# Row sums of a third head group by accumulating transfers, with a new instruction order and buffers named in lists

## The chip, the cores and the metric

The kernel runs on one core of a Trainium2 chip. A core has five engines that run side by side, each with its own queue of instructions that it takes in order: TensorE (PE, matrix products into the PSUM memory), VectorE (DVE, element-wise work and statistics), ScalarE (ACT, functions of one input), GpSimd (POOL, here small operations and the issue of some transfers) and SyncE (SP, here only the issue of transfers). Transfers (DMA) run on 16 engines that all queues share. Engines wait for one another through semaphores.

The metric is the device time of one execution in microseconds. Before the change it is 3014.59 us, the median of three runs (3012.68 to 3015.29).

## The reference

There are 32 graphs of 512 nodes with 256 features. For each, two layers of masked attention over the same adjacency matrix are computed. Layer 0 is a whole transformer block (attention, layer norm, a two-layer perceptron of width 1024, layer norm) inside a residual and another norm; layer 1 is attention alone inside a residual and a norm. Cut to what matters here:

```python
allowed = (adj > 0) | (adj.T > 0) | eye            # layer 0; layer 1: adj != 0
scores = einsum('hqd,hkd->hqk', q * scale, k)      # 8 heads of 32
attn = softmax(where(allowed, scores, -inf), -1)
ctx = einsum('hqk,hkd->hqd', attn, v)
x = layernorm(x + ctx @ Wo.T + bo)
ff = relu(x @ W1.T + b1) @ W2.T + b2               # layer 0 alone
```

The softmax is computed as exp(scores), multiplied by the mask, divided by its sum over the keys. That row sum, 512 queries by 8 heads for each layer of each graph, is what the change moves.

## The kernel before

Everything of a graph is held transposed: scores have the keys on the 128 partitions and the queries along the free side. A layer of a graph is worked in eight steps `k`, two head groups `hg` of four heads by four blocks of 128 keys. A step has four parts. `scores(layer, k)` (line 404) writes the four heads' scores into the one PSUM tile `s`. `exp` (line 413) has ScalarE write their exponentials into an SBUF tile `p` of 128 x 2048 fp32, of which there are eight. `masked` (line 417) has VectorE multiply it by the mask. `product` (line 424) has TensorE multiply it by the values, summing over the four key blocks of a group in the PSUM tile `acc`.

The row sums go another way, to spare TensorE. After a product, `pair(layer, k)` (line 437) has GpSimd issue a transfer of 1 MB that adds tile `k + 1` onto tile `k`. `fold` (line 440) is the same addition on VectorE. Per layer there are three pairs, (0,1), (2,3) and (4,5), and three folds: 0 onto 2 ends group 0 in tile 2; 6 + 7 into tile 3 and then 4 onto tile 3 end group 1 in tile 3 (whose own content was summed by then). So one tile per group, `2 + hg`, holds sums over four key blocks, and what is left is the sum over 128 partitions. There are two ways for that:

- `sums` (line 448): TensorE multiplies the tile by a matrix of ones, four matmuls into a PSUM tile `psR`, which comes out already spread over 32 partitions a head; `blocks` (line 489) has VectorE transpose it in blocks of 32.
- for groups that are in `SPREAD`: two accumulating transfers (`halve`, line 464) add the upper half of the partitions onto the lower, 128 to 64 and 64 to 32. Four copies (`spread`, line 469, on SyncE's queue) put the four heads next to each other on the partitions of the tile `part`, of which there is one. `blocks` transposes that, and `reduce` (line 493) sums the 32 values on VectorE.

In both cases `invert` (line 498), `widen` (line 506) and `divide` (line 510) follow on VectorE, and `guard` (line 502) on GpSimd adds the sums to a running total that is looked at once, at the end. Then `project` (psO) and the rest of the layer follow. `SPREAD` holds (layer 0, group 0) and (layer 1, group 0). The last graph's layer 1 has no transfers at all: its `sums` takes the four tiles of a group straight, 16 matmuls, which `final` decides.

The order of all work is written out by hand as three lists of calls, which are issued as they stand: `opening` (five graphs), `period` (run 26 times, each time for five neighbouring graphs, `a` the oldest, `c` in the middle of its layer 0 and its perceptron, `d` at its first attention, `e` being loaded), and `closing`. A call puts its instructions at the end of its engine's queue, so that a list is an order for each of the five queues. A list therefore says both what follows what on an engine and, roughly, what stands beside it on the others.

Buffers come from pools. A tile is named by a tag and a key, and the pool hands out the buffers of a tag in turn (`p` has eight, `y` four, `x`, `xT`, `v`, `kT` two). Only the three PSUM banks for dense products are named one by one, in a string of digits, `banks`. A new tile in a buffer waits for all readers of the old one. Dense products (line 162) are made either `wide`, one matmul with 128 columns, or as four matmuls with 32 columns each, which lie side by side in the array.

Of the kernel before, what the change touches and what calls it, by code (L numbers as in the profile page):

```python
# [27 lines left out]
def kernel(ctx: ExitStack, tc: tile.TileContext, t: dict, out: bass.AP):  # L28
# [15 lines left out]
    P = 128  # L44
# [106 lines left out]
    def plain(pools: ExitStack):  # L151
# [7 lines left out]
        def dense(out, lhsT, rhs, start, stop, wide):  # L159
# [4 lines left out]
        SPREAD = {(0, 0), (1, 0)}  # L164

        banks = iter(
            "012012021021122121012012010210210210201012102021121021012012012012102102102102102020120122021201212101120120212010"
            + "120121212010121212012012120120021212102101010212101010210210102102201010" * 13
            + "102120201210021021010210102102102021201021010210202101201201210210212102102102121021021021021021202102120120"
        )  # L170
# [5 lines left out]
        class Graph:  # L176
# [6 lines left out]
            def at(self, tag, n, shape, dtype=F32, **kw):  # L183

                key = (tag, n)
                if key not in self.tiles:
                    name = f"{tag}_{self.b}" + "".join(f"_{i}" for i in (n if isinstance(n, tuple) else () if n is None else (n,)))
                    pool = small if tag in SMALL else ps_s if tag == "s" else ps_a if tag == "acc" else work
                    self.tiles[key] = pool.tile([P, *shape], dtype, tag=tag, name=name, **kw)
                return self.tiles[key]  # L190

            def bank(self, kind, n, shape):

                key = (kind, n)
                if key not in self.tiles:
                    name = f"ps{kind}_{self.b}" + "".join(f"_{i}" for i in n)
                    self.tiles[key] = ps_d.tile([P, *shape], F32, tag=f"d{next(banks)}", name=name, bufs=1)
                return self.tiles[key]

            def final(self, layer):  # L200

                return self.b == B - 1 and layer == 1
# [239 lines left out]
            def sums(self, layer, hg):  # L442

                ps = self.bank("R", (layer, hg), [N])
                folded = [2 + hg] if not self.final(layer) else range(hg * NQ, (hg + 1) * NQ)
# [11 lines left out]
            def spread_out(self, layer, hg):  # L457

                return (layer, hg) in SPREAD and not self.final(layer)

# [125 lines left out]
        def opening(a, b, c, d, e):  # L586
# [6 lines left out]
            b.flip(1)  # L593
            b.sort(1, 0, 0)
            a.entries()
            a.transpose(0, 0)
            a.transpose_out(0, 0)
            a.query_key(0, 0, 0, None, wide=True)
# [3 lines left out]
            b.cast()  # L602
            a.query_key(0, 1, 0, None, wide=True)
            a.query_key_out(0, 1, 0, None)
            a.entry(0)
            a.entry(2)
            a.masks(0)
            a.scores(0, 3)
            a.exp(0, 3)
            a.scores(0, 2)  # L610
            a.exp(0, 2)
            a.query_key(0, 1, 1, None)
            b.flip(0)
            a.scores(0, 0)
            a.exp(0, 0)
            a.masks(1)
            a.masks(2)
            a.value(0, 0)
            a.value_out(0, 0)
            a.scores(0, 1)  # L620
            b.sort(1, 0, 1)
            a.exp(0, 1)
            a.query_key(0, 0, 1, None)
            a.query_key_out(0, 1, 1, None)
            a.query_key_out(0, 0, 1, None)
            a.value(0, 1)
            a.masked(0, 0)
            b.sort(1, 1, 0)
            a.value_out(0, 1)
            a.masked(0, 1)  # L630
            a.scores(0, 5)
            a.exp(0, 5)
            a.constants(22, 23)
            a.product(0, 0)
            a.pair(0, 0)
            a.constants(4, 6)
            a.once(0)
            b.sort(0, 1, 0)
            a.product(0, 1)
            b.sort(0, 0, 0)  # L640
            a.masked(0, 2)
            a.constants(10, 12)
            a.masked(0, 3)
            b.sort(1, 1, 1)
            a.scores(0, 4)
            a.exp(0, 4)
            a.masked(0, 4)
            a.scores(0, 6)
            b.sort(0, 1, 1)
            b.join(0, 1)  # L650
            a.exp(0, 6)
            a.product(0, 2)
            a.scores(0, 7)
            a.exp(0, 7)
            a.masked(0, 7)
            a.product(0, 3)
            a.context(0, 0)
            b.join(1, 0)
            b.sort(0, 0, 1)
            a.pair(0, 2)  # L660
            a.fold(0, 2, 2, 0)
            a.product(0, 4)
            a.once_out(0)
            a.bias(1)
            b.join(0, 0)
            b.entry(0)
            b.value(0, 0)
            b.join(1, 1)
            b.query_key(0, 1, 0, None)
            a.halve(0, 0, P // 2)  # L670
            b.query_key(0, 0, 0, None)
            b.query_key_out(0, 0, 0, None)
            b.query_key_out(0, 1, 0, None)
            b.query_key(0, 1, 1, None)
            b.scores(0, 0)
            b.value(0, 1)
            a.halve(0, 0, P // 4)
            b.exp(0, 0)
            a.masked(0, 5)
            a.product(0, 5)  # L680
            b.value_out(0, 1)
            b.query_key(0, 0, 1, None)
            a.masked(0, 6)
            b.scores(0, 2)
            a.fold(0, 3, 6, 7)
            a.product(0, 6)
            a.product(0, 7)
            a.pair(0, 4)
            b.exp(0, 2)
            a.fold(0, 3, 3, 4)  # L690
            a.constants(20, 22)
            b.query_key_out(0, 1, 1, None)
            a.constants(6, 8)
            a.spread(0, 0, 0)
            b.query_key_out(0, 0, 1, None)
            b.scores(0, 3)
            a.spread(0, 0, 1)
            b.exp(0, 3)
            a.spread(0, 0, 3)
            a.spread(0, 0, 2)  # L700
            b.entry(2)
            a.blocks(0, 0)
            a.reduce(0, 0)
            b.scores(0, 7)
            b.exp(0, 7)
            a.constants(17, 20)
            a.sums(0, 1)
            a.blocks(0, 1)
            a.invert(0, 1)
            a.once(2)  # L710
            a.guard(0, 1, 0)
            a.invert(0, 0)
            a.widen(0, 1)
            a.context(0, 1)
            a.divide(0, 1)
            a.constants(8, 10)
            b.entry(1)
            a.widen(0, 0)
            a.divide(0, 0)
            a.project(0, 0, wide=True)  # L720
            b.scores(0, 5)
            a.add(1, 1)
            b.value_out(0, 0)
            c.flip(1)
            a.add(1, 0)
            a.stats(1, 1)
            b.exp(0, 5)
            b.entry(3)
            a.project(0, 1)
            c.cast()  # L730
            b.entries()
            a.stats(1, 0)
            a.aggregate(1, 1)
            a.constants(12, 14)
            a.aggregate(1, 0)
            c.sort(1, 0, 0)
            a.once_out(2)
            a.root(1, 0, 2)
            a.center(1, 0)
            a.affine(1, 0)  # L740
            b.scores(0, 1)
            a.center(1, 1)
            a.affine(1, 1)
            a.add(1, 3)
            a.add(1, 2)
            a.stats(1, 2)
            b.masks(0)
            a.stats(1, 3)
            c.sort(1, 1, 0)
# [2157 lines left out]
```

## Time and profile before

| | |
|---|---|
| median of three runs | 3014.59 us |
| the profiled execution's own time | 3012.29 us |
| its span, first to last instruction | 3010.5 us |
| TensorE, VectorE, ScalarE, GpSimd busy | 2959.1, 2707.0, 1746.2, 972.2 us |
| granted TensorE clock, mean over the span | 0.995 |
| one period of the middle part | 91.58 us |
| transfers | 391.22 MB, 130 GB/s on average |

The profile is of one execution on the chip. A row of a group has the line of the kernel, the engine, the operation, what is written and read, the number of instructions after an x, then the busy time in total, the mean time of one in ns, and the idle time of the engine just before such instructions with what ended it. A matmul in fp32 shows as two instructions of about equal length. Matmuls overlap, and their ends are modelled, so the busy time of TensorE says little on how closely the blocks follow; the starts in a timeline do. A row of the timeline has start, length, engine, line, operation, tiles, and the number of instructions that were merged.

### The profile page before, as it was taken

What the parts mean: (1) busy time and instruction counts of PE and PEld (TensorE: products, weight loads), DVE (VectorE), ACT (ScalarE), POOL (GpSimd) and SP (SyncE); (2) the same over time, 40 slices, a digit from 0 to 9 for tenths busy, and PEclk for the clock granted to TensorE, in tenths of its full rate; (3) what the DMA queues carried; (4) which work ended last, traced back from release to release, by engine and by line L of the source; (5) the groups of instructions that cost most, each with busy time, mean ns of one, the idle gap of its engine ahead of it and who ended that gap; (6) DMA issues with size and microseconds to landing.
All of it is one profiled execution on the core that took longest, in us unless ns stands there. A gap on an engine that the chain in (4) does not pass through costs nothing.

```text
span 3010.5 us, 82999 instructions
## 1 busy us (share of the span) xinstructions
PE 2959.1 (98%) x36442; PEld 1375.9 (46%) x36442; DVE 2707.0 (90%) x3588; ACT 1746.2 (58%) x2111; POOL 972.2 (32%) x1252
## 2 busy tenths in 40 slices
PE   7989999999999999999999999999999999999997
PEld 2544445544444444445444445444454444454443
DVE  4879999999999999999999999999999999998996
ACT  4446655566565566565566655665655665556654
POOL 0222433233333233333233332333332333323241
PEclk9999999999999999999999999999999999999999
DMA  7867767676666676676666666766666776767560
GB/s 157 137 118 134 140 130 138 128 144 126 135 136 126 129 146 134 131 137 125 137 135 135 132 132 127 147 127 132 134 130 130 145 132 128 137 127 136 102 113 27
DMA packets 277169, 391.22 MB, mean 130 GB/s; under 512 B 153376, under 2 KB 237472, under 8 KB 246048
## 3 DMA queue, kind: packets, MB, share of 16 engines
q0 software_dynamic: 36304, 264.53, 47.6%
q1 hardware_dynamic: 240496, 121.32, 18.4%
q8 instruction: 288, 4.72, 0.7%
q14 instruction: 81, 0.66, 0.1%
HBM read 72.23 MB, written 33.55 MB: 35 GB/s over the span
## 4 chain that ended last, share of the span: by engine, by line
PE 93%; DVE 3%; DMA 2%; ACT 1%; issue 1%; POOL 1%; SPq 0%; DVEq 0%; POOLq 0%; ACTq 0%
PE s L404 17%; PE psF L162 14%; PE acc L424 14%; PE psH L162 14%; PE psQK_None L162 11%; PE psV L162 7%; PE psO L162 7%; PE psQK L162 4%; PE psT L365 2%; PE psR L448 2%; DMA p<-p 1%; DVE p L417 1%; ACT p L413 1%; DVE p L440 1%; DMA w_L_gnn_Wqkv<-in_L_gnn_Wqkv_dram 0%
## 5 line engine op out<-in xcount | busy, mean ns | idle before, releaser
L413 ACT ACTIVATE p<-s 128x2048 f32<-128x2048 f32 x512 | 963.0, 1881 | 496.2 <-PE s L404 459.8
L417 DVE TENSOR_TENSOR p<-p,m 128x2048 f32<-128x2048 f32 x512 | 1162.5, 2278 | 49.9 <-ACT p L413 46.7
L404 PE MATMUL s<-qT,kT 32*64 32x512 f32 x8192 | 572.7, 615 | 22.7 <-ACT p L413 21.4
L424 PE MATMUL acc<-p,v 128*32 128x512 f32 x4096 | 507.7, 596 | 1.6 <-ACT cT L433 1.5
L162 PE MATMUL psH<-xT,w_L_gnn_W 128*32 128x256 f32 (+1 forms) x6200 | 471.2, 380 | 1.5 <-DVE bov L321 1.5
L162 PE MATMUL psF<-w_L_gnn_W,hT 128*32 128x256 f32 (+1 forms) x6704 | 459.9, 380 | 0.0
L440 DVE TENSOR_TENSOR p<-p,p 128x2048 f32<-128x2048 f32 x189 | 431.0, 2281 | 10.7 <-DMA p<-p 9.4
L539 POOL TENSOR_SCALAR rs<-mv 128x2 f32<-128x2 f32 (+1 forms) x320 | 196.5, 614 | 726.6 <-DVE mv L534 713.3
L162 PEld LDWEIGHTS psH<-xT,w_L_gnn_W 128*32 128x32 f32 (+1 forms) x6200 | 302.7, 119 | 199.1 <-issue 55.3
L540 POOL TENSOR_TENSOR rs<-rs,neg_half 128x2 f32<-128x2 f32 (+1 forms) x320 | 369.7, 1155 | 26.7
L162 PEld LDWEIGHTS psF<-w_L_gnn_W,hT 128*32 128x32 f32 (+1 forms) x6704 | 291.2, 116 | 178.8 <-ACT hT L575 32.6
L437 POOL DMA_DIRECT2D p<-p x189 | 174.1, 921 | 530.0 <-PE acc L424 460.4
L575 ACT ACTIVATE hT<-psH,c_L_gnn_b 128x256 f32<-128x256 f32 x512 | 211.4, 474 | 200.0 <-PE psH L162 200.0
L404 PEld LDWEIGHTS s<-qT,kT 32*64 32x64 f32 x8192 | 119.5, 130 | 335.4 <-issue 113.2
L464 POOL DMA_DIRECT2D p<-p x126 | 107.8, 855 | 464.5 <-DVE mv L534 196.2
L162 PE MATMUL psQK_None<-xT,w_L_gnn_Wqkv 128*32 128x512 f32 (+1 forms) x2012 | 246.5, 598 | 5.6 <-DMA w_L_gnn_Wqkv<-in_L_gnn_Wqkv_dram 4.7
L162 PE MATMUL psO<-w_L_gnn_Wo,cT 128*32 128x256 f32 (+1 forms) x2776 | 241.8, 381 | 1.8 <-DVE cT L510 1.8
L424 PEld LDWEIGHTS acc<-p,v 128*32 128x32 f32 x4096 | 119.7, 110 | 253.0 <-issue 187.9
L162 PEld LDWEIGHTS psO<-w_L_gnn_Wo,cT 128*32 128x32 f32 (+1 forms) x2776 | 155.3, 123 | 99.2 <-issue 45.6
L370 ACT COPY xT<-psT 128x512 f32<-128x512 f32 x130 | 76.0, 585 | 198.9 <-PE psT L365 198.8
L560 ACT ACTIVATE x<-z,ms,rs 128x256 f32<-128x256 f32 x128 | 73.2, 597 | 167.2 <-DVE ms L544 164.0
L531 DVE BATCH_NORM_STATS2 st<-y 128x6 f32<-128x256 f32 x384 | 155.0, 422 | 6.2
(77 smaller groups left out, 2845.3 us busy)
## 6 DMA issues: line engine op xcount, KB each, us to landing
p<-p POOLq DMA_DIRECT2D x189, 1024.0 KB, 7.9
p<-p POOLq DMA_DIRECT2D x63, 512.0 KB, 5.9
x<-in_x_dram SPq DMA_DIRECT2D x32, 512.0 KB, 4.2
code<-in_adj_dram POOLq DMA_DIRECT2D x32, 512.0 KB, 5.9
m<-code SPq DMA_DIRECT2D x32, 512.0 KB, 4.9
out_dram<-x SPq DMA_DIRECT2D x32, 512.0 KB, 6.2
p<-p POOLq DMA_DIRECT2D x63, 256.0 KB, 6.3
part<-p SPq DMA_DIRECT2D x252, 64.0 KB, 2.0
```

The lines of the kernel that those rows point to most:

```text
L162: nc.tensor.matmul(out[at], lhsT[:, at], rhs, start=start, stop=stop)
L404: nc.tensor.matmul(s[half * P // 2 : (half + 1) * P // 2, j, :], self.kT(layer)[at, hg, key : key + P // 2], self.qT(layer)[at, hg, :], st ...
L413: nc.scalar.activation(self.p(layer, k), self.at("s", (layer, k), [HPC, N]), AF.Exp, scale=SCALE)
L417: nc.vector.tensor_tensor(p, p, m[:, k % NQ, None, :].to_broadcast([P, HPC, N]), ALU.mult)
L424: nc.tensor.matmul(acc[j * HD : (j + 1) * HD, :], self.v(layer)[:, kc, h * HD : (h + 1) * HD], self.p(layer, k)[:, j, :], start=(kc == 0), ...
L437: nc.gpsimd.dma_start(out=self.p(layer, k), in_=self.p(layer, k + 1), accum_op=ALU.add)
L440: nc.vector.tensor_tensor(self.p(layer, dst), self.p(layer, a), self.p(layer, b), ALU.add)
L464: nc.gpsimd.dma_start(out=p[:rows], in_=p[rows : 2 * rows], accum_op=ALU.add)
L531: nc.vector.bn_stats(self.at("st", (n, i), [6]), self.y(n, i))
L539: nc.gpsimd.tensor_scalar(rs, self.mv(n)[:, a:b, 1:2], EPS, None, ALU.add)
L540: nc.gpsimd.tensor_tensor(rs, rs, neg_half[:, a:b, None], ALU.pow)
L575: nc.scalar.activation(self.hT(h)[:, f, :], ps[:, f % 2, :], AF.Relu, bias=b1[:, f : f + 1])
```

## The change

`SPREAD` gets a third group, layer 1's second: after `fold(1, 3, 3, 4)` its tile is halved twice by transfers and copied out, and the sum over partitions no longer runs on TensorE. `final` becomes `direct` and is true of the first graph's layer 0 too: both its head groups are summed on TensorE from the four tiles each, and its pairs, folds, halvings and copies are taken out of the opening. All three lists of calls are written anew. Besides the moved calls they differ in the place of nearly every call, and in some products being wide that were not, or the reverse. And where the pools handed out buffers in turn, strings of digits now name the buffer of each new tile of eleven tags; the numbers of buffers stay.

```diff
-        SPREAD = {(0, 0), (1, 0)}
-
-        banks = iter(
-            "012012021021122121012012010210210210201012102021121021012012012012102102102102102020120122021201212101120120212010"
...
+        SPREAD = {(0, 0), (1, 0), (1, 1)}
+
+        slots = {
...
+            "p": iter(
+                "012345670231647523756401721046531063547261724530615340273247605142016537136745026"
+                + "352401721476053410365273267450162514037134760524302651721674503615340273247605142016537136745026" * 4
+                + "35240175604172365423701574135267423165046057123"
+            ),
...
                     pool = small if tag in SMALL else ps_s if tag == "s" else ps_a if tag == "acc" else work
+                    if tag in slots:
+                        tag, kw = f"{tag}_{next(slots[tag])}", {"bufs": 1}
                     self.tiles[key] = pool.tile([P, *shape], dtype, tag=tag, name=name, **kw)
...
-            def final(self, layer):
-
-                return self.b == B - 1 and layer == 1
+            def direct(self, layer):
+
+                return (self.b, layer) in ((0, 0), (B - 1, 1))
...
-                folded = [2 + hg] if not self.final(layer) else range(hg * NQ, (hg + 1) * NQ)
+                folded = [2 + hg] if not self.direct(layer) else range(hg * NQ, (hg + 1) * NQ)
...
-                return (layer, hg) in SPREAD and not self.final(layer)
+                return (layer, hg) in SPREAD and not self.direct(layer)
```

Of the period, the calls that close layer 1's second group, as they stand in the old and in the new list (between them, where a line of dots stands, come calls of other work):

```
old                             new
b.product(1, 5)                 b.product(1, 5)
b.pair(1, 4)                    b.scores(1, 6)
...                             ...
...                             b.masked(1, 6)
b.product(1, 7)                 b.fold(1, 3, 6, 7)
...                             d.scores(0, 3)
b.fold(1, 3, 6, 7)              b.pair(1, 4)
...                             ...
b.fold(1, 3, 3, 4)              b.fold(1, 3, 3, 4)
b.bias(2)                       b.halve(1, 1, P // 2)
...                             ...
b.sums(1, 1)                    b.halve(1, 0, P // 2)
...                             ...
b.blocks(1, 1)                  b.halve(1, 1, P // 4)
b.guard(1, 1, 0)                ...
b.invert(1, 1)                  b.spread(1, 1, 2), and three more
...                             ...
b.widen(1, 1)                   b.blocks(1, 1)
...                             ...
b.divide(1, 1)                  b.reduce(1, 1)
...                             ...
b.project(1, 0, wide=True)      b.invert(1, 1), b.widen(1, 1), b.divide(1, 1)
b.project(1, 1, wide=True)      ...
                                b.project(1, 1, wide=True)
                                ...
                                b.project(1, 0, wide=True)
```

Of the opening, graph 0's layer 0 from its last exp on:

```diff
 a.masked(0, 6)
+a.sums(0, 0)
 a.context(0, 0)
+a.blocks(0, 0)
+a.reduce(0, 0)
+a.invert(0, 0)
...
-a.pair(0, 2)
-a.fold(0, 2, 2, 0)
...
-a.halve(0, 0, P // 2)
-a.halve(0, 0, P // 4)
...
-a.fold(0, 3, 6, 7)
-a.fold(0, 3, 3, 4)
...
-a.spread(0, 0, 0)
...
 a.sums(0, 1)
```

At the very end, one call of `guard` stood between the last graph's two calls of `root` (line 539, two operations on GpSimd); in the new list none stands there, and three stand behind the last store.

## The prediction

> **What bounds the kernel now.** I began with the page's parts 1 and 2, to see which engine is full and where it isn't.
>
> ```profile
> span 3010.5 us, 82999 instructions
> PE 2959.1 (98%) x36442; PEld 1375.9 (46%) x36442; DVE 2707.0 (90%) x3588; ACT 1746.2 (58%) x2111; POOL 972.2 (32%) x1252
> ...
> PE   7989999999999999999999999999999999999997
> ```
>
> TensorE is full but for 51.4 us (3010.5 - 2959.1), which lie in the first and last slices; VectorE is second at 90%. As a busy TensorE may hide stalls under its pipelined matmuls, I asked for the busy times of chosen stretches: the opening, one steady period, and the closing.
>
> ```profile
> core 0: us, PE busy (x) PEld busy (x) DVE busy (x) ACT busy (x) POOL busy (x), PEclk, DMA share, GB/s
> 0.00:50.00 50.00, 32.57 (x304) 10.84 (x308) 16.15 (x10) 24.19 (x22) 3.87 (x13) 0.95 0.78 177
> 50.00:100.00 50.00, 44.14 (x416) 22.53 (x412) 32.53 (x46) 19.38 (x23) 6.25 (x10) 0.91 0.90 140
> ...
> 1337.90:1429.48 91.58, 91.58 (x1121) 43.04 (x1124) 84.74 (x113) 54.55 (x67) 33.76 (x42) 1.00 0.67 133
> ```
>
> A period lasts 91.58 us (the same query-key block starts at 1337.90, 1429.48, 1521.06), all of it TensorE. VectorE has 6.84 us left in it. The timeline of TensorE in such a period gives what a block costs, from its start to the next start, rather than by its modelled end:
>
> ```profile
> 1436.74 1.11 PE L404 MATMUL s<-qT,kT 32*64 32x512 f32 x16
> 1437.78 1.07 PE L448 MATMUL psR<-p,ones 128*32 128x512 f32 x8
> 1438.66 1.90 PE L162 MATMUL psQK_None<-xT,w_L_gnn_Wqkv 128*32 128x512 f32 x16
> ```
>
> A row-sum block (four matmuls, eight instructions) holds TensorE for 0.88 us; the period's other one (1482.94 to 1483.80) for 0.86. Adding the blocks of a period in this way leaves no hole: the steady stretch is bound by TensorE's work alone. So the change is priced as TensorE work in the 26 periods, provided the others keep up, and as waits in the ends. The durations needed come from the groups and DMA issues:
>
> ```profile
> L417 DVE TENSOR_TENSOR p<-p,m 128x2048 f32<-128x2048 f32 x512 | 1162.5, 2278 | 49.9 <-ACT p L413 46.7
> L440 DVE TENSOR_TENSOR p<-p,p 128x2048 f32<-128x2048 f32 x189 | 431.0, 2281 | 10.7 <-DMA p<-p 9.4
> L448 PE MATMUL psR<-p,ones 128*32 128x512 f32 x568 | 73.6, 598 | 0.1
> L493 DVE TENSOR_REDUCE total<-sT 128x16 f32<-128x512 f32 x63 | 43.2, 686 | 2.2
> L464 POOL DMA_DIRECT2D p<-p x126 | 107.8, 855 | 464.5 <-DVE mv L534 196.2
> p<-p POOLq DMA_DIRECT2D x63, 512.0 KB, 5.9
> p<-p POOLq DMA_DIRECT2D x63, 256.0 KB, 6.3
> part<-p SPq DMA_DIRECT2D x252, 64.0 KB, 2.0
> ```
>
> 568 instructions are 71 blocks: 32 of layer 0, 31 of layer 1, 8 of the last graph's direct sums.
>
> **What the Trainium skill says.** "Perfetto Trace Analysis", Identifying the Most-Contended Engine, warns that matmul busy share is no good measure of how near TensorE is to its limit; the start-to-start reading above is my answer to it, and it confirms the 98%. "TensorE: Matmul & The Clock Gate", Part 3, The mechanism, says that matmuls on different tiles of the array run concurrently; the trace agrees (eight instructions of 598 ns in 0.88 us). So four 32-column matmuls count as one wide one, and the narrow/wide swaps of the new order are nearly free. "DMA: Bandwidth & Descriptors", Issuing engines are not separate DMA queues, says that transfers of all engines share the same 16 DMA engines; here they are busy 0.67 of the period, so 0.75 MB more per graph is not free of delay, but has room.
>
> **The change, part by part.**
>
> *Row sums of layer 1's second head group leave TensorE.* 31 graphs lose one block: 31 x 0.87 = 27.0 us, 26 x 0.87 = 22.6 of it in the periods.
>
> *Graph 0, layer 0, goes straight on TensorE.* Group 0 gains four blocks and group 1 has four for one: 7 x 0.87 = 6.1 us more (the last graph's four blocks took 2983.79 to 2987.25, 3.46, which is the same rate). Three transfers, two halvings, four copies and three additions on VectorE (3 x 2.28 = 6.8 us) go. Net on TensorE: -20.9 us. Row-sum instructions fall from 568 to 47 blocks x 8 = 376.
>
> *VectorE* gets 31 reductions, 31 x 0.686 = 21.3 us, minus the 6.8: about +14. In a period 84.74 becomes 85.4 against 90.7, so 5.3 us stay free. Covered as long as its waits for others fit in those 5.3 us.
>
> *GpSimd and transfers.* 62 more halvings at 0.855 us on GpSimd, 1.7 us a period of some 33; four more copies on SyncE's queue, some 0.63 us each by its timeline (two took 1.25), 2.5 us a period. They add 24 MB to the 264.5 MB of the software queue, whose packets take 47.6% of the engines: +4%. On GpSimd the second halving waits for the first to land (5.9 us), with a reciprocal square root and another group's halving issued between; behind it stand only guards until the next root. On SyncE, the next graph's flip and sort stand behind the copies, and their joins come 30 us of TensorE work later.
>
> *The new chain's length.* Halvings 5.9 + 6.3, copies 4 x 0.63 + 2.0, then transpose, reduce, reciprocal, widen, divide on VectorE (0.70 + 0.69 + 0.25 + 0.71 + 0.68): about 20 us behind the addition that starts it. In the new list 42 us of TensorE work stand between that addition and the projection. Hidden; if its cover went, the projection would be late and TensorE with it.
>
> *All orders are new.* Adding the start-to-start times in the listed order gives a period shorter by 0.85 to 0.88, so the new neighbours cost nothing themselves: 16 score blocks stand apart in both, and wide for narrow moves no more than 0.02 a block. I then went through the places where an input is due soonest. Scores need their one PSUM tile back from exp (1.89 us plus about 0.2 of latency): the tightest pair has a query-key block and a transpose between, 2.3 us; met by some 0.2. The last transpose of layer 2's input comes 7.8 us behind the fourth MLP block; add, statistics, root, centring, root, norm take 7.5. The projection of layer 0 comes within a microsecond of its divide. So the list fits, with slack of tenths: I count 0, with 0.5 us a period (13 us) as the other end.
>
> *Named buffers.* There are still eight p tiles. Counting TensorE work between the last listed use of a tile and the exp that reuses it, the old rotation leaves 0.0 to 1.7 us at its tightest in the period, the new list 4.6. Where this ran out in the ends it cost TensorE time: exp stood for a transfer into p, and scores behind exp, for 8.5 us at 192.
>
> ```profile
> PE s L404 <- ACT p L413: 8.5, 1, 8.5
> ```
>
> *The ends.* Idle TensorE in the opening is 17.4 + 5.9 + 8.5 = 31.8 us, in the closing 19.6 (2.5, 1.1, 0.3, 5.5 and 10.3 after 3000). Waits of this kind are 3.0 us at 70.7, 8.5 at 192.1 and 2.5 at 2757.1: 14.0 together. Not all goes: in the new opening a tile comes 2.9 us after a transfer of 7.9 was issued into it. I take half, -7. In the first 70 us the chain shows transfers for graph 0's sums (7.3 and 9.6 us), which vanish, but graph 1 now arrives later to fill TensorE: -2. The last roots no longer have guards between them: -1. Ends -10, bounds -20 and +8.
>
> **Sum.** -20.9 - 10 = -31 us on the profiled execution: 3012.3 - 31 = 2981. Its time is 2.3 under the median of the runs, 3014.6; against that, 2984 us.
>
> **Rivals.**
> *Stalls of tenths (20%).* A late input in each period costs 0.3 to 0.8 us: the period is 91.0 to 91.5, and 8 to 21 us of the gain go: 2992 to 3005. For it: slacks of tenths, and transfers that landed in 6.9 to 11.9 us. Against: the old list was as tight and lost nothing.
> *VectorE becomes the bound, slower (13%).* It has 5.3 us free where 6.84 were idle. The addition that closes group 1 now stands 3.5 us of TensorE work behind the transfer it needs (25 before), which takes 7.9 to land; if VectorE keeps its old idle time, a period takes 85.4 + 6.8 = 92.2, 26 x 0.6 = 16 us more than before; with graph 0's 6.1 us, less 5 blocks of 0.87 in the ends, 3032, and 3022 if the ends gain their 10. It decides once VectorE waits more than 6.2 us a period (85.4 + 6.2 = 91.6). Against: by my count VectorE reaches that addition 1 to 2 us after the transfer has landed.
> *Nothing measurable (7%).* Periods gain 22 us, and a badly filled opening or stalls eat them: 3009 to 3020. That the work isn't removed is out: the blocks are gone from the list.
>
> **How the numbers follow.** My forecast, with its own range 2970 to 2992, has 60%. Together with the stalls 80% are faster by over 0.2% (6 us, about what a measurement of this kernel can tell), 7% within, 13% slower. The range leaves out the slower case and a little at the low end: 2970 to 3014.
>
> **What would show it.** Right: a repeating period near 90.7 us with TensorE busy throughout, 376 row-sum instructions, 93 reductions (63 + 31 - 1), VectorE near 85.4 us a period; TensorE idle below 45 us in all; no exp waiting 8 us for a transfer. Wrong: scores or projections with idle before them in every period, VectorE waiting for transfers into p in the middle of the span, or idle in the first 250 us above 32 us.

## The result, and the profile after

The changed kernel takes 3009.01 us (median of 12 runs, 2998.28 to 3019.2), the kernel before 3012.35 us beside it: a ratio of 0.9982, 95% interval 0.9968 to 0.9996 (the two medians alone give 0.9989). The change is worth 0.1 to 0.2%; the forecast was 1.0%. Ratios leave out runs over 1.5% above the fastest of the same kernel, which are two here, both of one experiment. The profiled execution took 3013.21 us, with a span of 3011.4 us.

The page's parts 1 and 2 of the kernel after answer to the first lines shown of before:

```profile
span 3011.4 us, 85356 instructions
PE 2949.1 (98%) x37234; PEld 1354.0 (45%) x37234; DVE 2710.1 (90%) x3617; ACT 1752.9 (58%) x2111; POOL 917.9 (30%) x1309
...
PE   8999999999999999999999999999999999999987
```

The first slices are fuller than before and the last emptier, and TensorE's busy time is only 10.0 us less, where 20.9 us of work were to go. The busy times by stretch (columns as before), with the same two stretches of the opening and one period:

```profile
0.00:50.00 50.00, 37.59 (x356) 12.70 (x360) 23.93 (x19) 21.61 (x18) 2.10 (x11) 1.00 0.72 174
50.00:100.00 50.00, 50.00 (x548) 28.60 (x544) 32.73 (x49) 25.25 (x31) 5.96 (x11) 1.00 0.47 93
1440.48:1531.57 91.09, 90.95 (x1160) 41.84 (x1164) 84.95 (x114) 54.84 (x66) 29.80 (x41) 1.00 0.80 146
```

The opening has 37.59 and 50.00 us of TensorE where it had 32.57 and 44.14. The period is the surprise. This one takes 91.09 us, others 90.8 to 93.0; the 25 intervals between the first hidden blocks of the perceptron, from 341.97 to 2631.92, average 91.60 us. Before, a period was 91.58. The first and the last of these blocks:

```profile
341.97 3.66 PE L162 MATMUL psH<-xT,w_L_gnn_W 128*32 128x256 f32 x64
2631.92 3.66 PE L162 MATMUL psH<-xT,w_L_gnn_W 128*32 128x256 f32 x64
```

A row-sum block is gone from each and nothing was saved. DMA engines are now busy 0.80 of the period, 0.67 before.

The work itself changed as listed. The groups of the row sums:

```profile
L502 PE MATMUL psR<-p,ones 128*32 128x512 f32 x376 | 47.5, 600 | 0.0
L543 DVE STREAM_TRANSPOSE sT<-part 128x512 f32<-128x512 f32 x93 | 65.2, 701 | 94.0 <-DMA part<-p 86.2 <-issue 6.9
L547 DVE TENSOR_REDUCE total<-sT 128x16 f32<-128x512 f32 x93 | 62.9, 676 | 2.6
part<-p SPq DMA_DIRECT2D x372, 64.0 KB, 2.9
```

There are 376 row-sum instructions (568 before) and 93 reductions (63). The new thing is line 543: VectorE stands 86.2 us for the copies into `part`. Before, it never waited for them in the periods. A copy's median landing is 2.9 us, 2.0 before.

Where does TensorE lose time, if it is busy 90.95 of 91.09 us? The waits of the 26 periods (310 to 2691 us; line, what for, us in total, times, longest) are, on TensorE and then on VectorE:

```profile
PE psO L162 <- DVE cT L564: 8.3, 14, 0.9
PE psT L419 <- ACT x L614: 5.1, 6, 1.7
```

```profile
DVE sT L543 <- DMA part<-p: 72.8, 27, 5.1
```

Over the same stretch of before, TensorE waited for nothing. The first list even understates it, because shorter stalls lie under the modelled ends of matmuls: from the last transpose's start to the next projection's start the median of the 26 periods is 0.89 us, the longest 1.54, where before it was 0.49. The projection (psO) waits for the divide (`cT`), and that stands behind the wait for the copies.

One period, in its order of time (start, length, engine, line, then a wait in brackets), shows how the copies come to be late. First VectorE reads `part` of group 1, then SyncE issues the four copies of group 0, GpSimd the next graph's 1 MB transfer, and VectorE waits:

```profile
1469.90 0.68 DVE L543 STREAM_TRANSPOSE sT<-part 128x512 f32<-128x512 f32 x1
1470.61 2.44 SPq L523 DMA_DIRECT2D part<-p  x4
1471.79 0.95 POOL L491 DMA_DIRECT2D p<-p  x1 [0.69 <-PE acc L478]
1479.85 0.71 DVE L543 STREAM_TRANSPOSE sT<-part 128x512 f32<-128x512 f32 x1 [2.22 <-DMA part<-p]
```

There is one tile `part`. Group 0's copies overwrite it, so they can't be issued before VectorE has read group 1's. By then it is so late that the last of the four goes out at 1472.5, 0.7 us behind the start of the 1 MB transfer's issue. How long these four copies took to land, by the trace's account of this tile from 1470.5 to 1473.2:

```profile
DMA to landing us min/median/max: 2.1/2.4/7.3
```

Three land in 2.1 to 2.6 us, and one, by the time at which VectorE's wait ends (1479.85) the last, in 7.3. This period is a mild one: it loses 0.3 us, and VectorE's wait is up to 5.1 us in others.

The closing loses the other half. Adding start-to-start costs in the listed order, the opening holds 283.9 us of TensorE work before and 286.4 after, in 330.4 and 309.8 us; the closing 276.9 and 275.9, in 299.0 and 320.2 us. So beyond its work at full speed TensorE spent 46.5 us in the old opening and 23.4 in the new, 22.1 in the old closing and 44.3 in the new.

Not all of this is standing still. Behind waits, and once behind a block of products with a single column, the traces show stretches of 3.4 or 6.8 us with half the TensorE clock: four in the old opening (20.4 us together) against one of 3.4 in the new, and none in the old closing, ahead of its last 10 us, against three (13.6 us) in the new. Most of such a stretch is busy, as the three in the new closing show (PE busy, then the clock behind the five engines):

```profile
2774.60:2777.80 3.20, 3.20 (x9) 2.49 (x9) 1.56 (x6) 0.16 (x1) 1.86 (x4) 0.50 0.46 143
2870.20:2876.80 6.60, 4.63 (x12) 3.34 (x13) 6.16 (x16) 3.32 (x4) 2.05 (x6) 0.50 0.00 1
2952.10:2955.30 3.20, 3.20 (x8) 2.58 (x9) 2.93 (x11) 0.00 (x0) 1.68 (x4) 0.50 0.00 0
```

At half the clock a score block of before took 1.90 us to the next start (at 80.8 us), elsewhere 1.04 (at 1436.7). If all work takes about twice as long, half of these 11 us of busy time, some 5.5 of the new closing's 44.3 us, go to the clock; in the old opening, with 15.8 us of busy time in its four stretches, some 8 of the 46.5. These are estimates. So a wait in the ends can be paid for a second time.

The chain of waits of after between 2895 and 2965 us (start, length, what) is transfers:

```profile
2925.30 5.10 DMA p<-p
2930.69 5.60 DMA p<-p
2939.02 2.64 DMA part<-p
2944.30 3.62 DMA part<-p
2952.05 3.63 PE psO L162 x8
```

These are the two halvings and the copies of graph 30's layer 1, with only the last graph left to work beside them.

In sum: opening -20.6, periods +0.3, closing +21.2, together the 0.9 us between the two spans of the profiled executions.

### The profile page after: what moved, and what is told of

It is laid out like the page before. It is cut to its first block, busy times and chain, and to the rows that moved or that the text cites. A ratio compares the mean times of both kernels' runs of the same rounds, so it can differ in the third digit from the quotient of the medians.

```text
span 3011.4 us, 85356 instructions
## 1 busy us (share of the span) xinstructions
PE 2949.1 (98%) x37234; PEld 1354.0 (45%) x37234; DVE 2710.1 (90%) x3617; ACT 1752.9 (58%) x2111; POOL 917.9 (30%) x1309
## 3 DMA queue, kind: packets, MB, share of 16 engines
q0 software_dynamic: 39712, 284.98, 52.8%
## 4 chain that ended last, share of the span: by engine, by line
PE 71%; DVE 16%; DMA 7%; issue 3%; ACT 2%; SPq 1%; POOL 0%; DVEq 0%; ACTq 0%
PE s L458 14%; PE psQK_None L162 11%; PE acc L478 11%; PE psH L162 10%; PE psF L162 7%; DVE p L471 6%; PE psV L162 6%; DMA part<-p 6%; PE psO L162 5%; PE psQK L162 3%; DVE st L585 2%; PE psT L419 1%; PE psR L502 1%; DVE x L384 1%; SPq L523 1%
## 5 line engine op out<-in xcount | busy, mean ns | idle before, releaser
L593 POOL TENSOR_SCALAR rs<-mv 128x2 f32<-128x2 f32 (+1 forms) x320 | 222.8, 696 | 954.7 <-DVE mv L588 950.8
L162 PE MATMUL psF<-w_L_gnn_W,hT 128*32 128x256 f32 x6704 | 459.6, 379 | 0.0
L494 DVE TENSOR_TENSOR p<-p,p 128x2048 f32<-128x2048 f32 x186 | 423.9, 2280 | 2.5 <-DMA p<-p 0.4
L518 POOL DMA_DIRECT2D p<-p x186 | 152.6, 823 | 775.2 <-DMA p<-p 303.1
L162 PEld LDWEIGHTS psH<-xT,w_L_gnn_W 128*32 128x32 f32 (+1 forms) x7952 | 258.5, 111 | 262.0 <-issue 66.3
L162 PEld LDWEIGHTS psF<-w_L_gnn_W,hT 128*32 128x32 f32 x6704 | 290.5, 116 | 178.4 <-issue 33.2
L491 POOL DMA_DIRECT2D p<-p x186 | 174.9, 940 | 255.4 <-PE acc L478 131.3
L594 POOL TENSOR_TENSOR rs<-rs,neg_half 128x2 f32<-128x2 f32 (+1 forms) x320 | 241.9, 756 | 26.7
L162 PEld LDWEIGHTS psO<-w_L_gnn_Wo,cT 128*32 128x32 f32 (+1 forms) x2632 | 164.6, 127 | 95.4 <-issue 21.7
L543 DVE STREAM_TRANSPOSE sT<-part 128x512 f32<-128x512 f32 x93 | 65.2, 701 | 94.0 <-DMA part<-p 86.2
```

The costliest lines, as they stand in the source:

```text
L162: nc.tensor.matmul(out[at], lhsT[:, at], rhs, start=start, stop=stop)
L491: nc.gpsimd.dma_start(out=self.p(layer, k), in_=self.p(layer, k + 1), accum_op=ALU.add)
L494: nc.vector.tensor_tensor(self.p(layer, dst), self.p(layer, a), self.p(layer, b), ALU.add)
L518: nc.gpsimd.dma_start(out=p[:rows], in_=p[rows : 2 * rows], accum_op=ALU.add)
L593: nc.gpsimd.tensor_scalar(rs, self.mv(n)[:, a:b, 1:2], EPS, None, ALU.add)
L594: nc.gpsimd.tensor_tensor(rs, rs, neg_half[:, a:b, None], ALU.pow)
```

## The experiments

Three theories of the periods. **One:** the single tile `part` makes group 0's copies wait for VectorE's read. **Two:** the shared DMA engines make them late, whatever the tile. **Three:** the new list is too tight by itself. For the opening: its gain comes from graph 0's direct sums (A), or from the new order and the named tiles (B).

### Two tiles for the copies

```diff
-                part = self.at("part", (layer, hg), [N], bufs=1)
+                part = self.at("part", (layer, hg), [N], bufs=2)
```

The same stands in `blocks`. To make room, the tiles `bov` are dropped and the bias is updated in place in `bo`.

> Changed kernel with two tiles for the gathered copies (part) instead of one; to make room for it, the two rows bov are written over the rows bo that they come from, once each. Theory 1 (one tile: the copies of layer 1's group 0 can only be issued once VectorE has read those of group 1 out of the single tile, and then come too late for it): VectorE's waits for copies in the periods fall from 73 us to under 10, the period from 91.6 to about 90.8, the time by about 20, to 2989. Theory 2 (shared engines: the copies are late because a 1 MB pair transfer starts a microsecond behind them): they are still beside that transfer, waits stay over 40 us, time 3000 or more. Theory 3 (the new list is too tight by itself, VectorE's wait is no cause): waits may fall, the time stays at 3005 to 3010.

Measured: 2985.65 us (2981.46 to 2988.57), ratio 0.9906 (0.9889 to 0.9922). Neither a wait of TensorE nor one of VectorE for `part` is left in the periods, and every period takes 90.82 us ((2615.72 - 345.28) / 25). The first and the last hidden block again, and one period by engine:

```profile
345.28 3.66 PE L162 MATMUL psH<-xT,w_L_gnn_W 128*32 128x256 f32 x64
2615.72 3.66 PE L162 MATMUL psH<-xT,w_L_gnn_W 128*32 128x256 f32 x64
```

```profile
1407.70:1498.50 90.80, 90.80 (x1164) 41.81 (x1156) 85.11 (x114) 54.85 (x67) 29.52 (x42) 1.00 0.82 146
```

Its DMA engines are busier than in the kernel after (0.82 to 0.80) and nothing is lost. The same steps as above now run in this order:

```profile
1463.71 2.77 SPq L523 DMA_DIRECT2D part<-p  x4
1464.56 0.68 DVE L543 STREAM_TRANSPOSE sT<-part 128x512 f32<-128x512 f32 x1
1466.47 0.95 POOL L491 DMA_DIRECT2D p<-p  x1 [0.70 <-PE acc L478]
1472.30 0.71 DVE L543 STREAM_TRANSPOSE sT<-part 128x512 f32<-128x512 f32 x1
```

The copies are issued before group 1's are read and before the 1 MB transfer, and the last line has no wait. Theory one holds for the periods: 26 x (91.60 - 90.82) = 20.3 us.

The two kernels have the same lists, so that their blocks on TensorE can be laid side by side, start to start. Over the 25 intervals the kernel after is 19.5 us longer, and all of it lies at two kinds of places: 11.5 us in front of and just behind the projection, and 8.0 us in front of transposes, which wait for the last step of a norm (line 614). No other block lost anything.

The closing still has 370.9 us from graph 28's first hidden block to the end, against 379.5.

### The 1 MB transfer later

One tile as in the kernel after; the transfer moves instead, behind a root (`c.root(3, 0, 2)`).

```diff
-            d.pair(0, 0)
             b.invert(1, 1)
...
             c.root(3, 0, 2)
+            d.pair(0, 0)
```

> Changed kernel with one call of the period moved: d.pair(0, 0) behind c.root(3, 0, 2), so that its 1 MB transfer starts about 6 us later, after the copies have landed; still one tile for the copies. Theory 1 (one tile): the copies are issued as late as before, their waits fall by a third at most, time about 3003. Theory 2 (shared engines): the copies land in about 3 us instead of 7, waits fall under 15 us, time about 2990. Theory 3: 3005 to 3010.

Measured: 3012.14 us (3003.82 to 3040.57, 20 runs), ratio 1.0006 (0.9989 to 1.0023): no gain. VectorE's wait for the copies is gone, but not the loss. The waits of VectorE, then of TensorE, from 310 to 2700 us:

```profile
DVE p L494 <- DMA p<-p: 69.0, 26, 11.7
```

```profile
PE s L458 <- ACT qT L448: 25.4, 4, 8.2
```

The copies were indeed late for the transfer ahead of them; that much of theory two is right. And in the profiled execution (3024.89 us, one of the longer) 21 of the 25 intervals take 90.8 to 91.5 us, nearly as with two tiles. The other four, of 97.8 to 101.8, hold 34.7 us of the loss: there the scores waited for the next graph's features, of which copies landed in up to 24.7 us. The transfer moved is itself late for its addition, 69 us over the periods, but outside these four VectorE waits no more than 2.6 us each time, and TensorE hardly loses by it. So moving the transfer cures the late copies too, and meets something else, which stands under "The third group undone".

### Both together

> Both edits together: two tiles for the copies, and the pair later. Theories 1 and 2 alike: no waits for copies left in the periods, period 90.7 to 90.8, time about 2988, no more than 3 us from the better of the two single edits. Theory 3: 3005 to 3010.

Measured: 2987.63 us (2985.79 to 2996.0), ratio 0.9923 (0.9906 to 0.9941), periods mostly 90.82. With two tiles the transfer's place matters no more than 2 us.

### Graph 0's direct sums alone

The kernel before, with graph 0's layer 0 straight on TensorE and its pairs, folds, halvings and copies taken out.

```diff
-                return self.b == B - 1 and layer == 1
+                return (self.b, layer) in ((0, 0), (B - 1, 1))
```

> Kernel before, with graph 0's layer 0 alone summed straight on TensorE (its transfers, additions, halvings and copies taken out of the opening, the rest of the order kept; group 0's row sums stand behind product 3). Theory A (the shorter opening of the changed kernel comes from these sums): 6 us more work, but the waits for transfers in the first 80 us go: opening shorter by 12 or more, time about 3000. Theory B (it comes from the new order of the opening and the named tiles): the opening stays within 5 us, time 3008 to 3018. The periods stay at 91.58 in both.

Measured: 3011.06 us (3007.13 to 3013.85), ratio 0.9992 (0.9983 to 1.0001). The first period's row sums start 1.7 us sooner (337.1, before 338.8). Seven blocks more on TensorE (6.1 us) cost nothing in an opening that idles, and gain next to nothing. B holds as far as this goes: the sums alone don't give the 20 us of the opening, so these come with its order and tiles. Whether the new order needs the sums wasn't tried.

### Group 1's copies read sooner

One tile again. VectorE takes the transpose of `part` ahead of one mask product.

```diff
-            d.masked(0, 4)
             b.spread(1, 1, 1)
...
             b.blocks(1, 1)
+            d.masked(0, 4)
```

> One tile part stays, but VectorE reads group 1's copies one mask (2.3 us) sooner, so that group 0's copies can be issued about 2.3 us sooner, in front of the 1 MB transfer of the next graph instead of behind its start. Theory 1 (the one tile makes the second group's copies wait for VectorE's read, and it is only this that is late): periods of 90.8 to 91.0 us, VectorE no longer waiting for the copies, 2985 to 2993 us in all, nearly as with two tiles. Theory 2 (any copy beside the 1 MB transfer is late, and the second tile helped in another way): waits shrink little, 3000 to 3010. Theory 3 (the list is too tight by itself): no change, 3006 to 3012.

Measured: 2993.34 us (2991.76 to 3000.02), ratio 0.9947 (0.993 to 0.9963). Every period takes 90.82 us:

```profile
1461.45 0.71 DVE L543 STREAM_TRANSPOSE sT<-part 128x512 f32<-128x512 f32 x1
1462.80 2.77 SPq L523 DMA_DIRECT2D part<-p  x4
1465.40 0.95 POOL L491 DMA_DIRECT2D p<-p  x1 [2.84 <-PE acc L478]
1471.41 0.71 DVE L543 STREAM_TRANSPOSE sT<-part 128x512 f32<-128x512 f32 x1
```

The copies are out when the 1 MB transfer starts, and no buffer was added. It is the same place by a second way: moving one call of 2.3 us gains 16 us. So the lateness needs both, the one tile that holds the copies back and the 1 MB transfer that they then meet. Only the closing, with its own list untouched, stays 4.4 us longer than with two tiles (375.3 to 370.9).

### The closing: graph 30's layer 1 on TensorE

From here on two tiles `part`. The last graph but one gets both groups of layer 1 by `sums`, and its first projection moves in front of the last graph's transpose.

```diff
-                return (layer, hg) in SPREAD and not self.direct(layer)
+                return (layer, hg) in SPREAD and not self.direct(layer) and (self.b, layer) != (B - 2, 1)
...
+            d.project(1, 0, wide=True)
             e.transpose(2, 0)
...
-            d.project(1, 0, wide=True)
```

> Two tiles part, and the last graph but one has layer 1's two groups summed by TensorE (two row-sum blocks, 1.8 us more of TensorE) instead of halvings and copies; its first projection moves in front of the last transpose. If the closing is long because the chain of halvings and copies of the last graphs has little other work beside it: TensorE's waits of 2.8 and 1.9 us before 2926 go, GpSimd's roots no longer stand behind halvings, closing 4 to 9 us shorter than with two tiles alone (312.3), 2977 to 2982 us in all. If the closing is long for the new order of the rest, or for a lower clock: 2985 to 2989 us.

Measured: 2982.31 us (2981.45 to 2985.91), ratio 0.9906 (0.9889 to 0.9922), 368.3 us from graph 28's first hidden block: 2.6 shorter, less than expected. Waits of 2.8 and 1.9 us before the last graph's transpose and projection went, but a new one of 2.1 us came: a query-key block of the last graph behind an addition (`y`) on VectorE.

### The third group undone

The kernel after, one tile, with the third group back on TensorE everywhere, the new order otherwise kept.

```diff
-            b.halve(1, 1, P // 2)
-            b.halve(1, 1, P // 4)
...
+            b.sums(1, 1)
             c.mlp(0)
+            b.blocks(1, 1)
             c.add(2, 0)
```

> The kernel after, one tile part, with the third group's sums back on TensorE (31 row-sum blocks more, 27 us of work; 62 halvings and 124 copies fewer). All else of the new order stays. Theory 1 (the copies behind one tile ate the gain): no waits for copies, period 90.8 + 0.87 = 91.7, about 3005 to 3014 us in all: the same as with the third group. Theory 3 (the new order loses some 0.8 us a period by itself): period 92.3 to 92.6, 3025 to 3035 us.

Measured: 3029.08 us (2996.87 to 3057.5, 14 runs), ratio 1.0048 (1.0025 to 1.0072). The profiled execution was the shortest: 2996.87 us, with all but one period 91.7 us, as theory one has it. So the new order isn't too tight (theory three falls), and its ends, with 2995.1 - 26 x 91.7 = 611 us, are 18 us shorter than those of before (3010.5 - 26 x 91.58 = 629). With the order held, a row-sum block is worth 91.68 - 90.82 = 0.86 us a period, and the new order by itself costs 91.68 - 91.58 = 0.10. But the other 13 runs are 11 to 61 us longer, which neither theory says. So it was run again:

> The kernel without the third group once more, for a second profile: its first one has 26 steady periods of 91.7 us and 2997 us, its median is 3029. If the same copies (group 0's, on SyncE's queue, in front of the next graph's 1 MB transfer) fall behind that transfer in the longer executions, VectorE waits for them by several us in many periods, these periods last 93 us or more, and the granted clock is lower there. If something else comes late, VectorE's waits for the copies stay below 3 us in all, and another wait fills the longer periods.

Measured: 3051.96 us. My expectation of late copies falls; VectorE doesn't wait for them at all. All periods take 91.7 us but two, of 118.5 and 120.5. TensorE's only wait from 300 to 2750 us, the transfers issued from 470 to 520 us (KB, median us to landing), and the stretches of the standstill:

```profile
PE s L458 <- ACT qT L448: 51.2, 2, 26.0
```

```profile
p<-p POOLq DMA_DIRECT2D x2, 1024.0 KB, 32.6
...
kT<-v SPq DMA_DIRECT2D x4, 64.0 KB, 28.8
...
m<-code SPq DMA_TRANSPOSE x2, 33.3
```

```profile
480.00:490.00 10.00, 9.17 (x52) 6.31 (x50) 4.98 (x11) 3.62 (x7) 2.12 (x4) 1.00 0.99 48
490.00:500.00 10.00, 0.00 (x0) 0.00 (x0) 0.00 (x0) 0.00 (x0) 0.00 (x0) 0.69 1.22 103
500.00:510.00 10.00, 0.00 (x0) 0.00 (x0) 0.52 (x1) 0.00 (x0) 0.00 (x0) 0.50 0.65 61
510.00:520.00 10.00, 5.58 (x48) 1.33 (x56) 9.97 (x8) 4.68 (x6) 2.82 (x4) 0.62 0.54 89
```

Transfers that land in 4 to 8 us elsewhere took some 30 us, all at once: two accumulating ones of 1 MB, two transposing ones of the mask, and the feature copies behind them. The DMA engines read as fully busy while they moved 48 GB/s, everything stood for 20 us, and the clock fell to 0.50. The two long periods are 26.8 and 28.8 us over, 55.6 together; the two profiled executions lie 55.1 us apart. That the other longer runs met the same is likely, but they were not profiled. In the second experiment's profile feature copies landed in up to 24.7 us and the 1 MB transfers in 21.7, in each of its four long periods: probably the same thing in small.

What sets one off is open, but the traces hold a lead. All six such events, four there and two here, begin where a transposing transfer of the mask is issued within 1 us of a 1 MB transfer; that transposing transfer lands in 13.3 to 17.3 us. Between 340 and 2690 us the profiled executions have 34 such meetings in the second experiment and 41 and 39 without the third group, but 6 before, 3 after and 13 with two tiles, where no transposing transfer took over 10.7 us. No experiment moved the transposing transfers alone, and most meetings are harmless, so that a meeting sets the standstill off is not shown. In the kernel after the longest feature copy and 1 MB transfer took 9.5 and 11.4 us, so its lost time there is not this.

### p tiles handed out in turn

Two tiles `part`; the list of digits for `p` taken out, so that the pool's own turn applies.

```diff
-            "p": iter(
-                "012345670231647523756401721046531063547261724530615340273247605142016537136745026"
-                ...
-            ),
```

> Two tiles part as before, but the p tiles are handed out by the pool in turn, not by the list of digits. If the named p tiles carry part of the gain, as the prediction's step on named buffers says: exp and scores wait for transfers into p, 3 to 10 us longer than with two tiles alone, 2989 to 2996 us. If the pool's turn does as well: 2983 to 2988 us. If the turn lands tiles still in use by a transfer in every period: over 3010 us.

Measured: 2990.35 us (2988.19 to 2996.11), ratio 0.9934 (0.9917 to 0.995), against 0.9906 with the list, whose interval touches it. Periods stay at 90.82 us. From graph 28's first hidden block it takes 375.6 us, 4.7 more than with the list; scores behind exp wait 7.4 us there instead of 3.5 (longest 4.1). The opening is not longer for it: graph 3's first hidden block starts at 341.73, with the list at 345.28 and, with one tile, 341.97. So the names of the `p` tiles are worth some 5 us, hardly clear of the noise, in the closing, and nothing in the opening or the periods.

### The closing again: the third group of the last graphs on TensorE

Two tiles; in the closing list only, graphs 28, 29 and 30 sum their third group on TensorE.

```diff
-                return (layer, hg) in SPREAD and not self.direct(layer)
+                return (layer, hg) in SPREAD and not self.direct(layer) and ((layer, hg) != (1, 1) or self.b < B - 4)
```

> Two tiles part, and in the closing list alone the third group of graphs 28, 29 and 30 back on TensorE (three row-sum blocks more, 2.6 us of work; six halvings and twelve copies fewer). The kernel without the third group had 360.9 us from graph 28's first hidden block to the end, the one with two tiles 370.9. If the chain of halvings and copies makes the closing long, the closing is 7 to 11 us shorter than with two tiles alone: 2974 to 2980 us in all. If the closing of the kernel without the third group was short for another reason (fewer bytes before it, another phase): 2984 to 2989 us.

Measured: 2974.57 us (2973.01 to 2977.95), ratio 0.9878 (0.9861 to 0.9894). The stretch from graph 28's first hidden block is 360.1 us, 10.8 shorter than with two tiles alone, though TensorE does 2.6 us more. Its longest waits from there on:

```profile
PE ps_total L2936 <- ACT x L614: 4.2, 1, 4.2
PE s L458 <- ACT p L467: 3.5, 10, 1.0
PE psO L162 <- DVE cT L564: 1.9, 2, 1.0
```

The transposes' waits for the last norm, 9.9 us in the closing of after and 5.9 with two tiles, are gone, and so are the closing's stretches at half clock before its last 10 us (17.1 us with two tiles, none here). Together with two tiles' 8.6 us (379.5 to 370.9) the 10.8 are most of the 21.2 us that the closing had lost. This is the fastest kernel of the study: it keeps the third group's transfers where TensorE is the bound and drops them where it isn't.

> As the kernel before it in this list, and graph 30's first group of layer 1 by TensorE too (one block more, 0.9 us; two halvings and four copies fewer). If every transfer on the last chain costs: 1 to 4 us shorter again, 2971 to 2979 us. If what the last graph waits for then is something else (its own statistics and roots): the same within 1 us.

Measured, with graph 30's first group on TensorE too: 2977.75 us (2974.87 to 2980.58), 361.4 us from the same point. No gain; TensorE's longest waits are the same two as above, 4.2 and 3.5 us, and no transfer is among them.

## Why the prediction was wrong

*Durations and counts:* right. A row-sum block was priced at 0.87 us and is worth 0.86 with the order held; the period fell by 0.76 (91.58 to 90.82) where nothing else was late, against a forecast of some 90.7, for the new order costs 0.10. The 24 MB of added transfers leave out graph 0's that go: 20.5 MB came (264.53 to 284.98). VectorE took 84.95 and 85.11 us against 85.4.

*The new chain's length, "Hidden":* this is the step that failed. It added 20 us for group 1's chain and set them against 42 us of cover, and it was group 0's chain that came late. The facts were there: the tile `part`, "of which there is one" in the kernel's description, and four copies more on SyncE's queue. The step priced the copies (0.63 each, landing 2.0) but not the tile's release, which it put at nothing. With two groups of the same graph in it, the second's copies wait for VectorE's read of the first, and that read stands behind five mask products. What they then met was the 1 MB transfer: 7.3 us to land, 72.8 us of waits of VectorE over the periods, and a period of 91.60 for 90.82. The question "who must have finished before this buffer may be written again" was asked of the `p` tiles alone.

*"The list fits, with slack of tenths":* the step allowed 0.5 us a period as its other end. The loss was 91.60 - 90.82 = 0.78 us, 20.3 in all, through a wait that was not on the list of tight places. The rival of stalls had this size and missed the cause. The rival in which VectorE becomes the bound by waiting for the 1 MB transfers falls: it waited 0.4 us for them in the periods of after. Where the transfer was moved, VectorE did wait 69 us, but in front of another addition (tile 0 onto tile 2 of layer 0, not the one that closes group 1), and the periods grew only where the features were late too.

*Room on the DMA engines:* right as a share (0.80 to 0.82 and no loss with two tiles), but a share says nothing on who stands behind whom.

*Named buffers:* the size, -7, is near the 5 us of the experiment by luck. The wait at 192 us that it counted on is gone with the tiles in turn as well (scores behind exp wait 2.0 us before 345 us, with and without the names), so it wasn't the names of the `p` tiles that took it away. And the count behind it was not sound. It took the old tiles to be reused in strict turn with 0.0 to 1.7 us to spare; under that turn 125 of 512 reuses would come before the last use, so the old pool can't have worked like that, though the description of the kernel before says so too, and the periods show no difference.

*The ends:* -10 was wrong in both parts. The opening lost 23 us of its time beyond work instead of 9, and not from graph 0's sums alone. The closing's grew by 22, which was not in the sum: the step looked for waits on `p` and for the roots at the end, and never asked what the third group's chain does where no other graph is left to cover it. The prediction's own rule for the period ("if its cover went, the projection would be late") applied there. Nor did the sum have a term for the half clock behind waits.

The sum of the forecast comes near the kernel that it had in mind: with two tiles `part` it takes 2985.65 us, forecast 2984. That is luck in part. Against before, that kernel's profile gains 19.8 us in the periods (forecast 22.6), and over 17 in the opening, where 9 were forecast, makes up for a closing that is still 13 us longer instead of 1 shorter. What came out is nearest to the rival "Nothing measurable" (7%): periods that gain 22 us, and stalls and a badly filled end that eat them, only that it was the closing and not the opening.

## What to carry to other kernels

When a second user is given to a single buffer, write down for each use who reads it last and when, and put the next writer's issue time there; its transfer may then fall behind a large one and pay for that too. Work moved from the bound engine to transfers pays only where other work covers its latency, so take such a change out again in the last stretch, where it costs (10.8 us here, a part of it through the lower clock). And when a sum of work and a measured period differ while the engine reads as busy, compare start-to-start times: the stall is under the modelled ends.

## What was not expected of the hardware

- A copy of 64 KB that went out 0.7 us behind the start of a 1 MB accumulating transfer's issue landed 7.3 us later; the three just ahead of it in 2.1 to 2.6 us.
- Rarely, transfers of several kinds stand still together: about 30 us to land for 64 KB copies, transposing transfers and 1 MB alike, with the DMA engines read as busy (0.99) at 48 GB/s at the start. In the one shown TensorE started nothing from 488.8 to 514.4 us; its clock was 0.50 from 493.7 to 517.6 us and then 1.00, so it came back 3.2 us after the work.
- Far shorter waits bring the half clock too: stretches of 3.4, 6.8 and, with two tiles, once 10.2 us, mostly behind waits in opening and closing, 17.1 us of them in that kernel's closing.
- TensorE read as busy for 90.95 of 91.09 us in a period that had 0.29 us more than the 90.80 without stalls. Over the 26 periods the waits shown are 13.4 us, where some 20 were lost; the rest is found only start to start, block by block against a kernel with the same list.
